# Five buffers for the exponentials of an attention block, with two small tiles moved into a shared region

## The chip, the cores and the metric

The kernel runs on one core of one Trainium2 chip. The metric is the device time of one execution in microseconds; three executions of the kernel before took 1975.81, 1975.38 and 1973.5, median 1975.38. A further execution was profiled: its time was 1972.27 and the span of its trace 1970.2.

## The reference, cut to what matters

The kernel computes one transformer block in which attention and the feed-forward part both read the normalized input. The input is 2048 tokens of 512 values; there are 16 heads of width 32; the feed-forward part has 4096 hidden units with weights packed in 4 bits.

```python
xn = _layernorm(x, axis=-1)
# attention
q, k, v = split(einsum('bsh,oh->bso', xn, w_qkv))      # 16 heads of 32
scores  = einsum('bhqd,bhkd->bhqk', q, k) / sqrt(32)
scores  = where(causal, scores, finfo.min)
probs   = softmax(scores, axis=-1)
attn    = einsum('bhqk,bhkd->bhqd', probs, v)
# feed-forward
inter   = gelu(xn @ Wg.T) * (xn @ Wu.T)
x = x + attn @ w_o.T + inter @ Wd.T
```

## The kernel before, in words

The kernel has an order of instructions written out by hand: each engine executes its instructions in the order in which the Python code issues them, and buffers are handed on by semaphore waits. Three stages follow each other.

**Projection and first maxima (0 to about 187 us).** The 16 token tiles of x are loaded, normalized (`normalize`, L489, into the tiles xn), turned with the identity matrix (`flip`, L505) and projected to q, k and v. Row maxima of the scores of the first two head pairs are taken.

**Attention, a pair of heads at a time (about 188 to 718 us).** Heads go in pairs, pair 0 to pair 7. For pairs 0 to 5 a loop runs over 40 steps a pair. A query block has 512 columns; the order of blocks is 1, 2, 3, 0, and block b has 4b + 4 key tiles of 128 rows. So steps 0 to 7 of a pair are block 1, steps 8 to 19 block 2, steps 20 to 35 block 3 and steps 36 to 39 block 0. Within a block the last four key tiles are diagonal: 4 to 7, 16 to 19, 32 to 35 and 36 to 39. Key tile 4 of block 2 is step 12, key tiles 4 and 8 of block 3 are steps 24 and 28. In each step, in this order:

- `score_cols` (L281) starts the scores of two heads in two PSUM banks of the pool ps_t (three banks) with the negated row maxima; `score_rows` (L210) computes scores of a later pair in two banks of ps_s (three banks); `add_scores` (L296) adds the products of keys and queries.
- `run_due` issues the values matmuls that earlier steps have put off (`add_values` L344, `add_rows` L355). `later_on` says by how many steps: for four full-width key tiles 0 to 3 in a row, the values of tile 0 are last read four steps after it was made.
- `exponentials` takes exp on ScalarE (ACT) from ps_t into a prob tile: two instructions of L310 in a full-width step. In a diagonal step the diagonal 128 columns are first clipped into the tile clip (L316), the rest goes to prob directly (L318), the clipped part is exponentiated into prob (L320) and `omit_later_keys` (L325) zeroes what lies above the diagonal on GpSimd (POOL).
- `maxima` (L234, L229) takes row maxima of the ps_s scores on VectorE (DVE), which frees these banks.
- `add_up` (L396, POOL) sums two prob tiles, so that row sums need half the matmuls. `keep_attention` (L430, L434 on ACT) copies a finished block out; `normalize_attention` issues one reciprocal (L445, DVE) and one product (L447, POOL) a step, up to four steps long, after a finished pair of pairs.

Some steps also hold a projection for a later group of heads (`project`, L166): eight matmul instructions of 3.7 us together, in steps 26, 28 and 30 of pairs 1 and 3 and in steps 5, 6, 14, 16 and 26 of pairs 2 and 4.

Pairs 6 and 7 run together (718 to 834 us, `exponentials_together`, L647), two prob tiles a step.

**Output projection and feed-forward (from about 834 us).** Pools of this part take the place of the attention's pools in SBUF, so some of its first loads wait for the last readers there. The SyncE queue issues all loads in order.

**Buffers.** prob comes from the pool probs with four buffers of 4 KB a partition, taken in turn; clip from a pool of its own with two buffers; the identity matrix ident from the pool of constants. A separate region, `turns`, holds 16 slots of 2 KB a partition with one buffer each, named by number: the tiles of x are in slots 0 to 7, the value weights in 8 to 11, the normalized tiles xn of the layer norm in 12 and 13; later the pair sums (`added`) are in 0 to 7, `both` in 8 and 9, and in the run of pairs 6 and 7 the low parts of the tokens in 0 to 15.

```python
tc.tile_pool(name="probs", bufs=4) as probs,
tc.tile_pool(name="clip", bufs=2) as clipp,
...
def turn_tile(i, name, dtype=F32, shape=(P, TB)):
    return turns.tile(list(shape), dtype, tag=f"turn{i}", name=name)
```

Of the kernel before, what the change touches and what calls it, by code (L numbers as in the profile page):

```python
# [38 lines left out]
F32 = mybir.dt.float32  # L39
# [7 lines left out]
P = 128  # L47
# [31 lines left out]
def block_kernel(  # L79
# [15 lines left out]
    def turn_tile(i, name, dtype=F32, shape=(P, TB)):  # L95
        return turns.tile(list(shape), dtype, tag=f"turn{i}", name=name)
# [17 lines left out]
    with (  # L114
# [3 lines left out]
        tc.tile_pool(name="vals", bufs=1) as vals,  # L118
        tc.tile_pool(name="tops", bufs=6) as topsp,
        tc.tile_pool(name="neg", bufs=8) as negp,  # L120
        tc.tile_pool(name="probs", bufs=4) as probs,
        tc.tile_pool(name="sums", bufs=5) as sump,
        tc.tile_pool(name="clip", bufs=2) as clipp,
        tc.tile_pool(name="qk", bufs=10) as qkp,
        tc.tile_pool(name="ps_s", bufs=3, space=PSUM) as ps_s,
        tc.tile_pool(name="ps_t", bufs=3, space=PSUM) as ps_t,
        tc.tile_pool(name="ps_m", bufs=1, space=PSUM) as ps_m,
    ):
        ident = const.tile([P, P], F32, tag="ident", name="ident")
        make_identity(nc, ident)  # L130

        mask_qk = const.tile([P, TB], F32, tag="mask_qk", name="mask_qk")
# [171 lines left out]
        def exponentials(p, n, tiles):  # L304
            qb, kt = steps[n]
            c0 = max(0, kt - 4 * qb) * P
            prob = probs.tile([P, 2, TB], F32, tag="prob", name=f"prob{p}_{n}")
            if kt < 4 * qb:
                for h, ps in enumerate(tiles):
                    nc.scalar.activation(prob[:, h, :], ps, AF.Exp)  # L310
                return prob


            clip = clipp.tile([P, 2, P], F32, tag="clip", name=f"clip{p}_{n}")
            for h, ps in enumerate(tiles):
                nc.scalar.activation(clip[:, h], ps[:, c0 : c0 + P], AF.Relu, scale=-1.0)  # L316
                if c0 + P < TB:
                    nc.scalar.activation(prob[:, h, c0 + P :], ps[:, c0 + P :], AF.Exp)  # L318
            diag = prob[:, :, c0 : c0 + P]
            nc.scalar.activation(diag, clip, AF.Exp, scale=-1.0)  # L320
            omit_later_keys(diag)
            return prob

        def omit_later_keys(diag):
            nc.gpsimd.affine_select(  # L325
                out=diag,
                in_=diag,
                compare_op=ALU.is_ge,
                fill=0.0,
                base=0,  # L330
                pattern=[[0, 2], [1, P]],
                channel_multiplier=-1,
            )
# [201 lines left out]
        for b in range(NTB):  # L535
            n = first[b]
# [34 lines left out]
        for m in range((NP - 2) * STEPS):  # L571
            p, n = divmod(m, STEPS)
# [7 lines left out]
            add_scores(p, n, ps)  # L580
            run_due(m)
            prob = exponentials(p, n, ps)
            maxima(ahead, n, ps_max)
            while full:
# [51 lines left out]
        def exponentials_together(p, n, tiles):  # L636
            if not diagonal(n):
                return exponentials(p, n, tiles)
            qb, kt = steps[n]
            c0 = (kt - 4 * qb) * P  # L640
            prob = probs.tile([P, 2, TB], F32, tag="prob", name=f"prob{p}_{n}")
            for h, ps in enumerate(tiles):

                nc.vector.tensor_scalar(
                    ps[:, c0 : c0 + P], ps[:, c0 : c0 + P], 0.0, None, ALU.min
                )
                nc.scalar.activation(prob[:, h, c0:], ps[:, c0:], AF.Exp)  # L647
            omit_later_keys(prob[:, :, c0 : c0 + P])
            return prob
# [433 lines left out]
```

## Time and profile before

| | us |
|---|---|
| median of three runs | 1975.38 |
| time of the profiled execution | 1972.27 |
| span of its trace | 1970.2 |
| TensorE busy / weight loads busy | 1934.5 / 1182.9 |
| VectorE / ScalarE / GpSimd busy | 1326.7 / 1104.2 / 927.6 |
| attention of pairs 0 to 5 | 188 to 718 |
| attention of pairs 6 and 7 | 718 to 834 |

A profile page gives the busy time of each engine, shares in slices, a chain of waits that ended last, and groups of instructions by line. Besides the page the trace answers questions: a table of waits (who waited for whom, in total, how often, the longest), and a timeline in order of time with start, length, engine, line, tile and form. In a timeline line, "x2" marks two like instructions drawn as one, and the square bracket tells how long the engine was idle before and what ended that. PE is TensorE, PEld its weight loads, DVE VectorE, ACT ScalarE, POOL GpSimd. The start of a matmul is recorded; its end is modelled.

### The profile page before, as it was taken

Reading aid. Unit: us, or ns where it says so; the run is one execution under the profiler, and the core shown is the slowest. Engines: PE = TensorE matmul, PEld = TensorE weight load, DVE = VectorE, ACT = ScalarE, POOL = GpSimd, SP = SyncE. Lnnn points to the kernel's source line nnn. Section 1 sums busy time; section 2 is a strip of 40 time slices with the busy share of each in tenths; the row PEclk is TensorE's granted clock in tenths of the full one; section 3 lists DMA queues with packets and bytes.
Section 4 is the critical chain, followed back from the end, with each engine's and each line's share of the span. In section 5 each row is a group of like instructions: output and inputs, shape, how many; then the busy total and the mean of one; then the engine's idle time right before and its main releaser. Section 6 shows DMA issues by size and latency. Waiting matters only on the chain.

```text
span 1970.2 us, 32411 instructions
## 1 busy us (share of the span) xinstructions
PE 1934.5 (98%) x11648; PEld 1182.9 (60%) x11648; DVE 1326.7 (67%) x2706; ACT 1104.2 (56%) x2299; POOL 927.6 (47%) x1055
## 2 busy tenths in 40 slices
PE   7999999999999999999999999999999999999998
PEld 3433333333333332247888888888888888888886
DVE  5657665656555764187777676777777777777774
ACT  2112665656556666625666666666666666666664
POOL 1001555545445653155655454555555555555451
PEclk9999999999999999999999999999999999999999
DMA  3000000000000000020000000000000000000002
GB/s 128 0 11 11 2 2 1 1 12 2 1 1 12 2 1 21 18 79 22 22 18 23 19 22 20 21 20 20 19 22 20 21 21 21 21 19 24 18 5 86
DMA packets 55392, 39.86 MB, mean 20 GB/s; under 512 B 14784, under 2 KB 47552, under 8 KB 55232
## 3 DMA queue, kind: packets, MB, share of 16 engines
q1 hardware_dynamic: 55232, 37.81, 6.5%
q8 instruction: 91, 1.49, 0.3%
q14 instruction: 69, 0.57, 0.1%
HBM read 33.55 MB, written 4.19 MB: 19 GB/s over the span
## 4 chain that ended last, share of the span: by engine, by line
PE 94%; ACT 3%; POOL 1%; issue 1%; DVE 1%; DMA 0%; DVEq 0%; ACTq 0%; POOLq 0%
PE gu L935 24%; PE gu L948 12%; PE pd L998 12%; PE av L344 10%; PE ps_s L210 8%; PE pd L1010 6%; PE ps_qk L166 6%; PE ps_t L281 4%; PE ps_t L296 3%; PE ps_v L516 3%; PE po L890 3%; ACT prob L310 2%; POOL added L396 1%; PE ptx L505 0%; PE pm L262 0%
## 5 line engine op out<-in xcount | busy, mean ns | idle before, releaser
L935 PE MATMUL gu<-xh,gu 128*128 128x512 f32 x1024 | 403.9, 394 | 0.0
L935 PE MATMUL gu<-lm,gu 128*128 128x512 f32 x1024 | 403.7, 394 | 0.0
L234 DVE TENSOR_REDUCE tops<-ps_s 128x1 f32<-128x512 f32 x384 | 243.7, 682 | 160.4 <-PE ps_s L210 122.3
L1019 DVE SCALAR_TENSOR_TENSOR acc<-pd,acc 128x512 f32<-128x512 f32 x512 | 317.1, 682 | 2.4 <-PE pd L1010 2.4
L980 POOL TENSOR_TENSOR parts<-inter,hi 128x512 fp32r<-128x512 f32 x128 | 171.1, 1336 | 278.2 <-DVE hi L976 271.9
L310 ACT ACTIVATE prob<-ps_t 128x512 f32<-128x512 f32 x384 | 205.7, 596 | 145.6 <-PE ps_t L296 102.1
L210 PE MATMUL ps_s<-qk,qk 32*128 32x512 f32 (+3 forms) x1280 | 286.4, 576 | 0.0
L948 PE MATMUL gu<-lm,gu 128*128 128x512 f32 x1024 | 279.7, 395 | 0.0
L972 DVE SCALAR_TENSOR_TENSOR inter<-gu,gate 128x512 f32<-128x512 f32 x128 | 88.5, 692 | 274.9 <-PE gu L948 274.9
L296 PE MATMUL ps_t<-qk,qk 32*128 32x512 f32 (+3 forms) x1280 | 271.2, 538 | 0.0
L1005 ACT ACTIVATE pd<-pd 128x512 f32<-128x512 f32 x512 | 263.4, 583 | 1.1 <-PE pd L998 1.1
L344 PE MATMUL av<-prob,v 128*32 128x128 f32 (+3 forms) x1856 | 257.6, 425 | 5.5 <-ACT both L430 4.2
L998 PE MATMUL pd<-wd,parts 128*128 128x512 f32 x1024 | 259.6, 396 | 0.0
L942 ACT ACTIVATE gu<-gu 128x512 f32<-128x512 f32 x256 | 148.7, 581 | 188.2 <-PE gu L935 188.1
L396 POOL TENSOR_TENSOR added<-prob,prob 128x512 f32<-128x512 f32 x144 | 179.6, 1268 | 115.9 <-ACT prob L310 115.4
L948 PEld LDWEIGHTS gu<-lm,gu 128*128 128x128 f32 x1024 | 192.0, 188 | 47.1 <-issue 0.2
L935 PEld LDWEIGHTS gu<-lm,gu 128*128 128x128 f32 x1024 | 191.9, 187 | 46.6 <-POOL wd L805 0.2
L998 PEld LDWEIGHTS pd<-wd,parts 128*128 128x128 f32 x1024 | 192.3, 188 | 45.8
L935 PEld LDWEIGHTS gu<-xh,gu 128*128 128x128 f32 x1024 | 192.0, 188 | 45.7 <-ACT wd L804 0.2
L344 PEld LDWEIGHTS av<-prob,v 128*32 128x32 f32 x1856 | 67.2, 108 | 206.2 <-issue 147.5
L229 DVE CUSTOM_DVE_ANT_0 ps_s<-ps_s,mask_qk 128x128 f32<-128x128 f32 (+3 forms) x256 | 120.8, 516 | 92.0 <-PE ps_t L296 52.3
L979 ACT CAST parts<-hi 128x512 fp32r<-128x512 f32 x128 | 79.7, 623 | 173.2 <-DVE hi L976 171.4
(106 smaller groups left out, 2942.8 us busy)
## 6 DMA issues: line engine op xcount, KB each, us to landing
pk<-packed SPq DMA_DIRECT2D x96, 128.0 KB, 2.2
sc<-scales SPq DMA_DIRECT2D x512, 8.0 KB, 1.6
x<-x SPq DMA_DIRECT2D x16, 256.0 KB, 3.5
acc<-x SPq DMA_DIRECT2D x16, 256.0 KB, 3.3
sc<-scales SPq DMA_DIRECT2D x256, 16.0 KB, 1.7
out<-acc SPq DMA_DIRECT2D x16, 256.0 KB, 2.2
wqk<-w_qk SPq DMA_DIRECT2D x4, 512.0 KB, 3.7
wv<-w_v SPq DMA_DIRECT2D x4, 256.0 KB, 5.4
```

The costliest lines, as they stand in the source:

```text
L210: nc.tensor.matmul(ps[:, :w], lhsT=qT[p // 2, qb][rows, i * P : (i + 1) * P], rhs=kT[p // 2, c][rows, :w], start=True, stop=True,)
L234: nc.vector.tensor_reduce(top, ps[:, :w], AX.X, ALU.max)
L296: nc.tensor.matmul(ps[:, c0:], lhsT=kT[p // 2, kt // 4][rows, (kt % 4) * P : (kt % 4 + 1) * P], rhs=qT[p // 2, qb][rows, c0:], start=False ...
L310: nc.scalar.activation(prob[:, h, :], ps, AF.Exp)
L344: nc.tensor.matmul(avs[p, qb][D * j : D * (j + 1), c0:c1], lhsT=v[kt // 4][:, kt % 4, D * head : D * (head + 1)], rhs=prob[:, h, c0:c1], s ...
L396: nc.gpsimd.tensor_tensor(t, prob_a[:, h], prob_b[:, h], ALU.add)
L935: nc.tensor.matmul(ps, lhsT=parts[:, i, k], rhs=mov, start=(k == 0 and i == 0), stop=(k == NK - 1 and i == 1),)
L948: nc.tensor.matmul(ps, lhsT=gu[g, m, j][:, 2, k], rhs=lm[b, k][1], start=False, stop=(k == NK - 1), skip_group_check=True,)
L980: nc.gpsimd.tensor_tensor(parts[:, 1], inter, high, ALU.subtract)
L998: nc.tensor.matmul(po, lhsT=parts[:, part, i * P : (i + 1) * P], rhs=w[:, part], start=(part == 0), stop=(part == 1),)
L1005: nc.scalar.activation(po, po, AF.Copy, scale=HIGH_SCALE)
L1019: nc.vector.scalar_tensor_tensor(acc[t], po, SUM_SCALE, acc[t], ALU.mult, ALU.add)
```

## The change

The pool of the exponentials gets a fifth buffer, and two small tiles leave their pools. The clipped scores use turn slots 12 and 13 by the parity of the step, where the normalized tiles xn of the layer norm were; the pool clip is gone. The identity matrix uses turn slot 14. The rest of the program, and the order of instructions on each engine, is the same.

```diff
-        tc.tile_pool(name="probs", bufs=4) as probs,
+        tc.tile_pool(name="probs", bufs=5) as probs,
         tc.tile_pool(name="sums", bufs=5) as sump,
-        tc.tile_pool(name="clip", bufs=2) as clipp,
...
-        ident = const.tile([P, P], F32, tag="ident", name="ident")
+        ident = turn_tile(14, "ident", shape=(P, P))
...
-            clip = clipp.tile([P, 2, P], F32, tag="clip", name=f"clip{p}_{n}")
+            clip = turn_tile(12 + n % 2, f"clip{p}_{n}", shape=(P, 2, P))
```

## The prediction

> **What bounds the kernel now.** I read the page first, then the table of waits for the stretch 186 to 720 us (pairs 0 to 5), then the timeline of single steps, because the first two turned out not to show the stall that matters.
>
> ```profile
> PE 1934.5 (98%) x11648; PEld 1182.9 (60%) x11648; DVE 1326.7 (67%) x2706; ACT 1104.2 (56%) x2299; POOL 927.6 (47%) x1055
> ```
>
> TensorE is busy 98% of the span at a granted clock of 0.999, so whatever the change brings must come out of TensorE's time. The two tiles that the change touches, prob and clip, live between 190 and 834 us; after that TensorE is busy without a gap (24.00 of 24.00 us from 836 to 860, 100.00 of 100.00 from 900 to 1000), so later stages only move along.
>
> ```profile
> ACT prob L310 <- PE av L344: 23.3, 18, 1.4
> ACT prob L310 <- POOL added L396: 16.5, 19, 0.9
> PE ps_t L281 <- ACT prob L310: 2.3, 3, 1.2
> ```
>
> These are idle us, times, and the longest. The first row is the wait that a fifth buffer can end: the exponentials of a step wait for the last values matmuls that read the buffer of four steps before. 18 times is 6 pairs by 3: key tile 4 of block 2, and key tiles 4 and 8 of block 3 (a quad's first tile is read until four steps later). The third row suggests that TensorE hardly cares. It is misleading, as the timeline of steps 28 and 29 of pair 0 shows (start, length, engine, line):
>
> ```profile
> 244.41 0.39 PE L281 MATMUL ps_t<-neg,ones_h 3*128 3x512 bf16 x2
> 245.07 0.59 PE L296 MATMUL ps_t<-qk,qk 32*128 32x512 f32 x2
> 246.05 0.39 PE L344 MATMUL av<-prob,v 128*32 128x256 f32 x2
> 246.11 1.09 ACT L310 ACTIVATE prob<-ps_t 128x512 f32<-128x512 f32 x2 [1.24 <-PE av L344]
> 246.38 0.75 PE L281 MATMUL ps_t<-neg,ones_h 3*128 3x512 bf16 x2
> 246.76 0.70 PE L210 MATMUL ps_s<-qk,qk 32*128 32x512 f32 x2
> 248.71 0.39 PE L281 MATMUL ps_t<-neg,ones_h 3*128 3x512 bf16 x2
> ```
>
> A step runs from one L281 pair to the next: 1.97 us for step 28, 2.33 for step 29. In step 28 the exponentials start 1.70 us after L281; in a step without the wait it is 1.34 (below: 332.10 to 333.44), so they are 0.36 late. The second L281 of step 29 takes the score bank that the first of these exponentials frees: ps_t has three banks, a step uses two. It starts 0.38 late, seen as a length of 0.75 instead of 0.39 and an L210 0.38 behind. Matmul ends are modelled, so this stall stands as busy time and is in no wait row. Now pair 1, where a projection of 3.7 us covers the same late exponentials:
>
> ```profile
> 328.46 3.70 PE L166 MATMUL ps_qk<-xnT,wqk 128*128 128x512 f32 x8
> 332.10 0.39 PE L281 MATMUL ps_t<-neg,ones_h 3*128 3x512 bf16 x2
> 333.44 1.08 ACT L310 ACTIVATE prob<-ps_t 128x512 f32<-128x512 f32 x2 [0.65 <-PE ps_t L296]
> 334.06 0.39 PE L281 MATMUL ps_t<-neg,ones_h 3*128 3x512 bf16 x2
> ```
>
> Step 29 is 1.96 us here: the trace of before contains the step without the stall. The first diagonal step of a block has it in a smaller form, since only the second instruction, L318, writes the prob tile:
>
> ```profile
> 300.34 0.28 ACT L316 ACTIVATE clip<-ps_t 128x128 f32<-128x128 f32 x1 [0.83 <-PE ps_t L296]
> 300.76 0.49 ACT L318 ACTIVATE prob<-ps_t 128x384 f32<-128x384 f32 x1
> 301.03 0.59 PE L281 MATMUL ps_t<-neg,ones_h 3*128 3x384 bf16 x2
> 302.98 0.28 PE L281 MATMUL ps_t<-neg,ones_h 3*128 3x256 bf16 x2
> ...
> 404.91 0.34 PE L281 MATMUL ps_t<-neg,ones_h 3*128 3x384 bf16 x2
> 406.62 0.28 PE L281 MATMUL ps_t<-neg,ones_h 3*128 3x256 bf16 x2
> ```
>
> Step 17 takes 1.95 us in pair 1 and 1.71 in pair 2, where a projection again covers the wait.
>
> [...]
>
> **The change part by part.** The sum is made against the profiled execution: span 1970.2, time 1972.27. The median of the runs is 1975.38, 3.1 above it; I carry the difference over.
>
> *Five prob buffers.* The order of instructions on every engine stays; only waits move: a tile waits for the readers of the tile five steps before instead of four. That work ends a whole step earlier at every place above, so ACT starts as soon as its scores are there (L296 plus 0.08). Then the second L281 is free within 0.02 to 0.03, as in steps without the wait. What is late next is VectorE: the second L210 takes the ps_s bank that the maxima of the step before free.
> - Full-width steps, VectorE early: step 13 of pair 0, step 25 of pairs 0, 2, 4, step 29 of pairs 0, 2, 4, 5: 8 x 0.36 = 2.9 us. (Step 29 of pairs 1 and 3 is covered already: 0.)
> - Step 13 of pairs 2 and 4: a reciprocal delays the maxima, so that L210's bank comes 0.15 after the step's start: 2 x 0.23 = 0.46.
> - Steps 13 and 25 of pairs 1, 3, 5: the same, with further reciprocals behind:
>
> ```profile
> 315.20 0.94 DVE L445 RECIPROCAL sums<-sums 128x128 f32<-128x128 f32 x1
> 316.06 1.22 DVE L234 TENSOR_REDUCE tops<-ps_s 128x1 f32<-128x512 f32 x2
> ```
>
>   Step 25 begins at 316.60 and the first maximum ends at 316.74 (0.68 each), so 0.23 is the upper end. VectorE is then a chain of maxima and reciprocals that does not get earlier, and the next two steps give back up to 0.2: lower end 0.03. I take 0.1, nearer to the chain: 6 x 0.1 = 0.6.
> - First diagonal steps: step 17 of pairs 0, 1, 3, 5 and step 33 of all six, 10 x 0.25 less 0.08 where VectorE is close = 2.4; step 5 of pairs 0, 1, 3, 5, 4 x 0.25 = 1.0; of pairs 2 and 4, VectorE bound, 2 x 0.07 = 0.14.
>
> Sum 2.9 + 0.46 + 0.6 + 2.4 + 1.0 + 0.14 = 7.5 us. Its lower end is 4.1 (the VectorE places at nothing, and 0.1 us lost again at each of the other 22, as L281's spread of 0.03 and VectorE's 0.06 together allow); its upper end is every stall whole: 16 x 0.38 + 16 x 0.27 = 10.4.
>
> *Pairs 6 and 7* (718 to 834 us) use two buffers a step and read them in the next step, before the exponentials that reuse them; no row there shows ACT waiting for L344. 0, and at most the 4.5 us in which L281 waits for exponentials there (3.1 and 1.4).
>
> *Clip in turn 12 and 13, ident in turn 14.* Same instructions. The clip tile's first wait is for the layer norm's last reader of these slots, over at 121.5 us, against 198.1 for the first clip; ident is written at 0.8 us into a fresh slot; low token parts enter these slots after 720 us, after the last clip at 716. Cover is over 4 us everywhere. Other tiles move in SBUF: L310 has 576 to 619 ns over four addresses now, so an address is worth less than 0.02 us an instruction either way, off the path: 0.
>
> *Waits elsewhere.* ACT loses 9 separate wait instructions and POOL 20, of 17 ns, beside other work: 0 to 0.5 us of gain, I take 0. Of the SyncE queue's transfers, one scale load before the feed-forward part waits for a prob buffer one step earlier (832.68 now); behind it queue accumulator loads, first needed over 10 us later. TensorE has no gap there: 0 either way. 18 weight loads of L281 get a wait for TensorE's own count; see the second rival.
>
> Result: 1972.27 - 7.5 = 1964.8 for a profiled execution, 1975.38 - 7.5 = **1967.9** for the median.
>
> **The rivals.** A difference below 0.2% (3.95 us) can't be told from none here.
>
> 1. *The score banks are the limit, not the prob buffers.* If exponentials were late for another reason (three ps_t banks, ACT's own queue), nothing changes: 1975.4. For it: what TensorE waits for is a PSUM bank. Against: in step 28 ACT is idle from 244.87, its scores end at 245.66 (245.07 + 0.59), and yet it starts only at 246.11, behind the L344 group that reads the old buffer. Half true would be where VectorE takes the stall over in most places: gain 2 to 4, 1972. [...]
>
> 2. *Slower: the new waits in TensorE's queue.* Each of 18 L281 weight loads waits for a score matmul of the step before. If such a wait emptied TensorE's pipeline, it would cost the score group in flight, 1.25 us from L281 to L296's end: 18 x 1.25 = 22.5, less 7.5: 1990. It decides from 0.64 us each, (7.5 + 3.95) / 18. Against: L210's weight loads wait for VectorE in every step and where that is over (244.43) they start without a gap; the matmul waited for ends about 0.7 us before the load is due (1.25 into a step of 1.97).
>
> 3. *Much faster: the second wait row too.* If ACT's waits for POOL were buffer waits, another 16.5 us would go: 1951. Against, the timeline of step 22 of pair 1:
>
> ```profile
> 310.35 0.68 PE L296 MATMUL ps_t<-qk,qk 32*128 32x512 f32 x2
> 311.11 1.09 ACT L310 ACTIVATE prob<-ps_t 128x512 f32<-128x512 f32 x2 [0.87 <-POOL added L396]
> ```
>
>   ACT starts 0.08 after its scores end at 311.03: the POOL end at 311.09 is a coincidence.
>
> **How the numbers follow.** Forecast (gain 4 to 10): 0.75. Rival 1: 0.16, of which 0.04 lies just over the 0.2% bound. Rival 2: 0.05. Rival 3: 0.04. Faster 0.75 + 0.04 + 0.04 = 0.83, same 0.16 - 0.04 = 0.12, slower 0.05. Range: from 1965.0 (the upper end of the sum, 10.4) to 1972.2 (into rival 1's half-true case), which leaves out under 2 in 10.
>
> **What would show it.** Right: step 29 of pair 0 at 1.97 us instead of 2.33, step 17 of pair 1 at 1.71; the row of ACT waiting for L344 gone; VectorE waits of L210 a little longer; gain spread evenly over pairs 0 to 5, none after 720 us. Wrong: step 29 still at 2.33, a gap before L281's weight loads in steps 5, 17 and 33, or the time before 186 or after 720 us changed.

## The result and the profile after

Six executions of the changed kernel have a median of 1966.26 us (1963.04 to 1968.42), six of the kernel before 1975.73 us: a ratio of 0.9954, with a 95% interval of 0.9944 to 0.9963. The forecast was 1967.9 with a range of 1965.0 to 1972.2. The profiled execution took 1963.04 us with a span of 1961.3 (before: 1972.27 and 1970.2). In the trace the line numbers below line 123 are one less than before, so L280, L209, L295, L309, L343 are the old L281, L210, L296, L310, L344.

The page again shows TensorE busy for 98% of the span. Its busy time fell by 8.6 us, though the change removes no matmul: what went was waiting that had stood inside the busy row.

```profile
PE 1925.9 (98%) x11648; PEld 1181.8 (60%) x11648; DVE 1325.1 (68%) x2706; ACT 1102.9 (56%) x2299; POOL 928.0 (47%) x1055
```

From the table of waits of the changed kernel for 185 to 715 us (idle us, times, longest):

```profile
ACT prob L309 <- PE ps_t L295: 97.7, 112, 1.2
...
ACT prob L309 <- POOL added L395: 14.7, 17, 0.9
...
PEld ps_s L209 <- DVE tops L233: 11.1, 35, 1.2
```

The row in which the exponentials waited for the values matmuls is gone. They now wait for their scores (L295), which is what should end last. The row with POOL is still there at 14.7 us: it was a coincidence, as the third rival's counter-argument said. The wait of L209's weight loads for VectorE, which was expected to grow a little, did not: 11.1 us in 35 waits, before 11.9 in 33.

For step 28 of pair 0 one line of the kernel before has to be added to those of the prediction: the group of L344 that reads the buffer of step 24 has 128 columns, and its last record ends, by the model, at 246.02, 0.09 ahead of the exponentials of 246.11.

```profile
245.59 0.63 PE L344 MATMUL av<-prob,v 128*32 128x128 f32 x10
```

The timeline of steps 28 and 29 of pair 0 in the changed kernel:

```profile
243.12 0.40 PE L280 MATMUL ps_t<-neg,ones_h 3*128 3x512 bf16 x2
...
243.78 0.60 PE L295 MATMUL ps_t<-qk,qk 32*128 32x512 f32 x2
...
244.31 0.63 PE L343 MATMUL av<-prob,v 128*32 128x128 f32 x10
...
244.46 1.08 ACT L309 ACTIVATE prob<-ps_t 128x512 f32<-128x512 f32 x2 [0.88 <-PE ps_t L295]
...
245.10 0.39 PE L280 MATMUL ps_t<-neg,ones_h 3*128 3x512 bf16 x2
...
247.06 0.39 PE L280 MATMUL ps_t<-neg,ones_h 3*128 3x512 bf16 x2
```

In step 28 the exponentials start at 244.46, 0.08 after their scores end (243.78 + 0.60) and 1.34 after the step began; before, it was 1.70. They no longer wait for L343: the group that reads the buffer of step 24 starts at 244.31 and its last record ends at 244.73, behind the start of the exponentials. The L280 of step 29 has its plain length of 0.39 again, and step 29 takes 1.96 to 1.97 us instead of 2.33. Step 17 of pair 1, a diagonal step, in the same view:

```profile
298.48 0.28 ACT L315 ACTIVATE clip<-ps_t 128x128 f32<-128x128 f32 x1
...
298.64 0.51 ACT L317 ACTIVATE prob<-ps_t 128x384 f32<-128x384 f32 x1
298.64 0.33 PE L280 MATMUL ps_t<-neg,ones_h 3*128 3x384 bf16 x2
...
300.34 0.28 PE L280 MATMUL ps_t<-neg,ones_h 3*128 3x256 bf16 x2
```

L317 follows L315 by 0.16 instead of 0.42, and the step takes 1.70 instead of 1.95. Before, only pairs 2 and 4 had that, under the cover of a projection.

The step lengths of the whole stage, from one L280 pair to the next, give the account. "Given back" is what the following steps became longer. No step outside this table changed by more than 0.05 us.

| place | instances | before, us | after, us | net gain, us |
|---|---|---|---|---|
| step 13 of pair 0; 25 of 0, 2, 4; 29 of 0, 2, 4, 5 | 8 | 2.33 | 1.97 | 2.9 |
| step 13 of pairs 2, 4 | 2 | 2.33 | 2.01 | 0.6 (0.03 each given back) |
| steps 13 and 25 of pairs 1, 3, 5 | 6 | 2.33 | 2.01 | 1.5 (0.03 to 0.09 each given back) |
| step 17 of pairs 0, 1, 3, 5; step 33 of all | 10 | 1.96 | 1.70 to 1.76 | 2.4 |
| step 5 of pairs 0, 1, 3, 5 | 4 | 1.96 (pair 0: 2.18) | 1.70 (1.91) | 1.0 |
| step 5 of pairs 2, 4 | 2 | 5.59 | 5.53 | 0.1 |
| step 9 of pair 3, a lone wait | 1 | 2.04 | 1.75 | 0.3 |
| all 240 steps | | 528.44 | 519.62 | 8.8 |

By pairs the gain is 1.83, 1.24, 1.32, 1.51, 1.32 and 1.59. Pairs 6 and 7 changed by 0.01 and the time after them by 0.02. Outside the span lie 1.74 us instead of 2.07: 8.9 of the span and 0.3 from there make the 9.2 between the two profiled executions; the medians are 9.5 apart.

### The profile page after: what moved, and what is told of

Read it like the earlier page. It is cut to its first block, busy times and chain, and to the rows that moved or that the text cites. A ratio compares the mean times of both kernels' runs of the same rounds, so it can differ in the third digit from the quotient of the medians.

```text
span 1961.3 us, 32383 instructions
## 1 busy us (share of the span) xinstructions
PE 1925.9 (98%) x11648; PEld 1181.8 (60%) x11648; DVE 1325.1 (68%) x2706; ACT 1102.9 (56%) x2299; POOL 928.0 (47%) x1055
## 4 chain that ended last, share of the span: by engine, by line
PE 94%; ACT 3%; POOL 1%; issue 1%; DVE 1%; DMA 0%; DVEq 0%; ACTq 0%; POOLq 0%
PE gu L934 24%; PE gu L947 12%; PE pd L997 12%; PE av L343 10%; PE ps_s L209 9%; PE pd L1009 6%; PE ps_qk L165 6%; PE ps_t L280 4%; PE ps_t L295 3%; PE ps_v L515 3%; PE po L889 3%; ACT prob L309 2%; POOL added L395 1%; PE ptx L504 0%; PE pm L261 0%
## 5 line engine op out<-in xcount | busy, mean ns | idle before, releaser
L209 PE MATMUL ps_s<-qk,qk 32*128 32x512 f32 (+3 forms) x1280 | 288.6, 576 | 0.0
L309 ACT ACTIVATE prob<-ps_t 128x512 f32<-128x512 f32 x384 | 205.9, 596 | 138.4 <-PE ps_t L295 121.5
L295 PE MATMUL ps_t<-qk,qk 32*128 32x512 f32 (+3 forms) x1280 | 266.9, 537 | 0.0
L343 PE MATMUL av<-prob,v 128*32 128x128 f32 (+3 forms) x1856 | 257.6, 425 | 5.5 <-ACT both L429 4.2
L343 PEld LDWEIGHTS av<-prob,v 128*32 128x32 f32 x1856 | 67.2, 108 | 206.2 <-issue 148.3
```

Source lines behind the costliest of these rows:

```text
L209: nc.tensor.matmul(ps[:, :w], lhsT=qT[p // 2, qb][rows, i * P : (i + 1) * P], rhs=kT[p // 2, c][rows, :w], start=True, stop=True,)
L295: nc.tensor.matmul(ps[:, c0:], lhsT=kT[p // 2, kt // 4][rows, (kt % 4) * P : (kt % 4 + 1) * P], rhs=qT[p // 2, qb][rows, c0:], start=False ...
L343: nc.tensor.matmul(avs[p, qb][D * j : D * (j + 1), c0:c1], lhsT=v[kt // 4][:, kt % 4, D * head : D * (head + 1)], rhs=prob[:, h, c0:c1], s ...
```

## The experiments

### The moves without the fifth buffer

```diff
-        tc.tile_pool(name="probs", bufs=5) as probs,
+        tc.tile_pool(name="probs", bufs=4) as probs,
```

> Four prob buffers, with clip and ident in the turn slots as in the change. Theory (the fifth buffer alone brings the gain): time as before, 1975.7 within 1.5 us; step 29 of pair 0 at 2.33 us, step 17 of pair 1 at 1.96, and ACT's wait for L344 back at 18 times and 23 us. Rival (the gain comes from where the tiles lie in SBUF or from the fewer wait instructions): 1966, step 29 at 1.97.

Measured: 1975.26 us (1972.41 to 1976.42), against 1974.99 for the kernel before in the same series; ratio 1.0 [0.999, 1.0009]. The step lengths that had fallen are back at their old values; only step 9 of pair 3 stays at 1.76. The wait row is back (18 waits and 23 us were expected), and so is the late start in step 28 of pair 0 (wait table, then timeline, of this kernel):

```profile
ACT prob L309 <- PE av L343: 21.9, 17, 1.4
```

```profile
247.36 0.39 PE L280 MATMUL ps_t<-neg,ones_h 3*128 3x512 bf16 x2
...
249.06 1.08 ACT L309 ACTIVATE prob<-ps_t 128x512 f32<-128x512 f32 x2 [1.24 <-PE av L343]
...
249.33 0.75 PE L280 MATMUL ps_t<-neg,ones_h 3*128 3x512 bf16 x2
...
251.66 0.39 PE L280 MATMUL ps_t<-neg,ones_h 3*128 3x512 bf16 x2
```

1.70 us into the step, an L280 of 0.75, a step of 2.33: the numbers of before. The new places of clip and ident and the shifted addresses cost and bring nothing; the gain comes with the fifth buffer. One part of the rival is not tested here: the smaller number of wait instructions also comes with the fifth buffer. ACT and POOL have 684 and 786 of them in this trace, 682 and 786 before, and 673 and 766 in the changed kernel. Against it speaks the table above, in which the steps that became shorter are, but for one, the stalled ones.

### The last reader a step earlier, with four buffers

The same wait can be ended from the other side: the old buffer's last read comes one step sooner, in the kernel before.

```diff
-                    later_on(3, attend_pair, p, n - 1, even, prob, 3 * P, TB)
+                    later_on(2, attend_pair, p, n - 1, even, prob, 3 * P, TB)
```

> The kernel before with four prob buffers; only the last values matmuls that read the first tile of a quad are issued one step earlier (three steps after the tile was made instead of four), so that the old buffer is free when its successor comes. Theory (it is this one reader that holds the buffer): steps 13, 25 and 29 of pair 0 fall from 2.33 to about 1.97, steps 5, 17 and 33 by about 0.25; with 0.3 us of matmuls moved from one step to the one before, the time comes to 1964 to 1969. Rival (a fifth buffer also ends other waits, those for POOL among them, or the score banks are the limit): 1973 to 1976.

Measured: 1969.86 us (1966.73 to 1972.04), ratio 0.9978 [0.9967, 0.9988]; 1964 to 1969 was expected. The wait for L344 is gone, so this reader did hold the buffer, yet less came than with the fifth buffer. The timeline of steps 28 and 29 of pair 0 shows where the rest stayed:

```profile
246.87 0.39 PE L281 MATMUL ps_t<-neg,ones_h 3*128 3x512 bf16 x2
...
248.21 1.09 ACT L310 ACTIVATE prob<-ps_t 128x512 f32<-128x512 f32 x2 [1.11 <-PE ps_t L296]
...
248.62 0.61 PE L281 MATMUL ps_t<-neg,ones_h 3*128 3x512 bf16 x2
...
250.81 0.39 PE L281 MATMUL ps_t<-neg,ones_h 3*128 3x512 bf16 x2
```

ACT is on time (1.34 into the step). But the moved matmuls took 0.22 us of TensorE's work out of step 28, which is now 1.75 long, and put it into step 27. ACT's pace has not changed: the first exponential frees its score bank some 1.95 us after the step's start. So the next L281 finds its second bank 0.22 late (a length of 0.61 instead of 0.39), and step 29 takes 2.19. A step with less work than that loop only waits in the next one. This is the score-bank limit of the first rival: real, but at about 1.97 us a step, just where the changed kernel's steps already are.

The small stalls show the same: steps 5, 17 and 33 fell from 1.96 to 1.93 only, where 0.25 less was expected. By the step lengths (without the first five steps of pair 0, where TensorE had about half its clock for a while, 0.66 on average from 190 to 200 us, see the last section) the stage is 5.6 us shorter than before. Only 2.0 of that is in steps 13, 25 and 29; 3.5 is in the fourth and fifth steps of the blocks, where the moved matmuls fill a wait of another kind. So the experiment shows what the exponentials waited for, but not what the wait was worth.

### The last reader a step later, with five buffers

```diff
-                    later_on(3, attend_pair, p, n - 1, even, prob, 3 * P, TB)
+                    later_on(4, attend_pair, p, n - 1, even, prob, 3 * P, TB)
```

> The changed kernel with five prob buffers; the last values matmuls that read the first tile of a quad are issued one step later (five steps after), which puts the same wait back, one step further on. Theory: ACT waits for L344 again; the stall of 0.36 to 0.38 us moves to steps 14, 26 and 30 (step 30 of pair 0 from 1.97 to about 2.33), the small one to steps 6, 18 and 34; time 1971 to 1976. Rival (five buffers help whoever reads last): 1966, no step longer than in the changed kernel.

Measured: 1975.23 us (1972.13 to 1976.06), ratio to before 1.0001 [0.9992, 1.0011]. The fifth buffer is cancelled, as expected. From the wait table of this kernel:

```profile
ACT prob L309 <- PE av L343: 22.2, 18, 1.5
```

The total came out, the division by steps only in part: steps 13, 25 and 29 without a projection take 2.39 to 2.44, since the moved 0.22 and the late bank meet there, and the steps behind them 2.10 to 2.11 and not 2.33: the long step has taken up most of the delay of its exponentials. The small stall did not move to steps 6, 18 and 34, which stayed at 1.43; steps 5, 17 and 33 take 2.13 where nothing else holds them, instead of 1.70. And as the moved matmuls leave the fifth steps of the blocks, those are shorter, so the near agreement of the total with the kernel before is in part chance. What these three experiments show is the wait itself: it goes and returns with the number of steps between a buffer's last read and its next use, from either side.

### VectorE's reciprocals apart from the late maxima

The prediction gave the odd pairs little since reciprocals stand among the maxima. Here the reciprocals of a finished block start no earlier than its sixth step:

```diff
-            if invert and kt < 4 * qb:
+            if invert and 5 <= kt < 4 * qb:
```

> The changed kernel; the reciprocals and products of finished blocks are issued only from key tile 5 of a block on, not at key tiles 0 to 4. Theory (where a reciprocal stands between two maxima, VectorE hands on the ps_s bank late and holds TensorE): step 24 of pairs 1, 3, 5 falls from 2.56 to about 2.26, step 12 of pairs 2 and 4 from 2.47 to 2.26, step 4 of pairs 2 and 4 from 2.58 to 2.12, and steps 13 and 25 of the odd pairs from 2.01 to 1.97; the steps that get the reciprocals grow by up to 0.04 each; sum -2.5 to -4 us, time 1962 to 1964. Rival (ScalarE's late exponentials set these steps anyway): 1966, step 24 of pair 1 still at 2.56.

Measured: 1962.04 us (1961.23 to 1962.9), ratio to before 0.9936 [0.9922, 0.9951], inside the expectation, and so is the stage by its step lengths, 3.3 us shorter than in the changed kernel. Step 13 and 25 of the odd pairs went from 2.01 to 1.97, so VectorE had only 0.04 left there. The larger part came in the step ahead: step 4 of pairs 2 and 4 from 2.58 to 2.12, step 12 of these pairs from 2.47 to 2.26. In the odd pairs, steps 12 and 24 went from 2.56 to 2.40 only, where 2.26 was expected: something else holds them too.

### The second copy of a finished block two steps later

In the fourth step of a block ACT has two copies (L429, L433) between the exponentials of two steps. The second copy and POOL's addition behind it are deferred, in the changed kernel:

```diff
-                    nc.scalar.copy(aT[og][qb][half], both[other])
-                    nc.gpsimd.tensor_tensor(
-                        aT[og][qb][half], aT[og][qb][half], both[half], ALU.add
-                    )
+                    later_on(2, join_halves, p, qb, both)
+                    return
...
+        def join_halves(p, qb, both):
+            nc.scalar.copy(aT[og][qb][half], both[other])
+            nc.gpsimd.tensor_tensor(
+                aT[og][qb][half], aT[og][qb][half], both[half], ALU.add
+            )
+            if p % 2 == 1:
+                invert.extend((og, qb, i) for i in range(4))
```

> Changed kernel, but ScalarE's second copy of a finished block (L434) and GpSimd's addition behind it come two steps later, so that in the fourth step of a block only one copy stands between the exponentials of two steps. Theory (ScalarE hands the score banks over late in that step, and VectorE's reciprocals are not what makes the fourth step of a block and the next one long): the 18 fourth steps (2.71 us now) become 0.2 to 0.4 us shorter and step 12 and 24 of pairs 0, 2, 4 (2.26) come near 1.97; 18 x 0.3 = 5.4 us, median 1959 to 1963. Rival (VectorE or the matmuls themselves set these steps): the copy is idle time on an engine that is not the bound, and the copy that comes two steps later delays exponentials there: 1966, or up to 2 us more.

Measured: 1959.73 us (three executions at 1959.71 to 1959.74, one at 1965.01), ratio to before 0.9932 [0.9915, 0.995]. Steps 23 and 24 of pair 1, first in the changed kernel:

```profile
308.68 0.81 PE L280 MATMUL ps_t<-neg,ones_h 3*128 3x512 bf16 x2
...
310.06 0.62 ACT L433 COPY aT<-both 64x512 f32<-64x512 f32 x1
...
310.70 1.08 ACT L309 ACTIVATE prob<-ps_t 128x512 f32<-128x512 f32 x2
...
311.39 0.82 PE L280 MATMUL ps_t<-neg,ones_h 3*128 3x512 bf16 x2
...
313.96 0.42 PE L280 MATMUL ps_t<-neg,ones_h 3*128 3x512 bf16 x2
```

and then with the copy deferred:

```profile
308.14 0.81 PE L280 MATMUL ps_t<-neg,ones_h 3*128 3x512 bf16 x2
...
309.88 1.08 ACT L309 ACTIVATE prob<-ps_t 128x512 f32<-128x512 f32 x2 [0.39 <-PE ps_t L295]
...
310.85 0.54 PE L280 MATMUL ps_t<-neg,ones_h 3*128 3x512 bf16 x2
...
312.96 0.39 PE L280 MATMUL ps_t<-neg,ones_h 3*128 3x512 bf16 x2
```

The exponentials of step 23 start 1.74 after the step's start instead of 2.02, the L280 of step 24 is 0.54 instead of 0.82 long, and step 24 takes 2.11 instead of 2.57. The median is as expected, but the place is not: the fourth steps (308.14 to 310.85) stayed as they were in all 18 instances (2.71, and 3.19 in step 3 of pair 0), so ACT's copies don't set them. One part of their length shows in both traces: the second L280 of this step starts 0.43 behind the first (0.91 in step 3 of pair 0), before either copy begins. In the second trace that is at 308.57, 0.05 behind the first exponential of step 22, whose single record ends at 308.52. Steps 21 and 22 take 1.75 and 1.76, less than the 1.97 of the loop of exponential and score bank, and the lag ends up here. What sets the rest of the step was not tried.

The size came in part by luck. By the step lengths the stage is 3.5 us shorter than in the changed kernel, where 5.4 was expected. The medians differ by 6.5, since three of these four executions have a mean clock of 1.0 and only two of the six of the changed kernel have; between executions at 1.0 (1959.71 and 1963.05) it is 3.3.

The edit also holds back the reciprocals of these blocks, which wait behind the deferred addition. The share of the copy alone is the difference between the version with late reciprocals and the version with both (below): 0.14 us in steps 12 and 24 of even pairs, 0.28 in odd ones, 2.6 in all.

### The table of the exponential loaded early

Executions of one kernel come in groups some 2 to 3 us apart (the six of the changed kernel at 1963.04 and 1963.06, 1966.24 to 1966.31, and 1968.42), which a gain of 9 us has to be told from. The last section deals with the cause; this edit tests it. A tiny exponential is put ahead, so that its function table isn't loaded at 188.7 us, where the load takes 1.28 us and TensorE sits idle for 1.19. First it was put among the projections (behind the layer norm's last statistics), in the changed kernel and in the kernel before:

```diff
+            if b + 2 == NTB:
+                warm_exp = small.tile([P, 1], F32, tag="warm_exp", name="warm_exp")
+                nc.scalar.activation(warm_exp, ones[:, :1], AF.Exp)
```

> Changed kernel plus one tiny exponential (128x1) on ScalarE right after the layer norm's last statistics, so that the table of the exponential is loaded there, under the projections, and not at 188.8 us, where its 1.28 us stand on the path while TensorE has nothing to do. Theory A (the gap at the load is what halves TensorE's clock for 6.827 us in some executions, at about 2.7 us each time): the load leaves 188.8 us, the stage starts 1.2 to 1.3 us earlier, and no execution has the stretch, so that the runs lie together near 1962 instead of in clusters at 1963.0, 1966.3 and 1968.4; median 1961 to 1963. Rival B (the stretch comes whatever stands there): the load's 1.3 us go and the clusters stay, median near 1965. Rival C (the load is hidden by other waits): 1966.3, no difference.

> The kernel before, with the early load of the exponential's table alone. Theory A (gap at the load triggers the half clock): 1971 to 1972 without clusters, and the ratio to the changed kernel with the same edit gives the gain of the fifth buffer without that noise: 8.8 us by the step lengths. Rival B: 1974 with clusters. Rival C: 1975.5, no difference.

Measured: 1964.93 us (1964.17 to 1965.23) for the changed kernel with it, 1973.89 (1972.74 to 1975.6) for the kernel before with it; ratios to before 0.9949 [0.9934, 0.9964] and 0.9995 [0.9985, 1.0004]. Both medians missed theory A (1961 to 1963, and 1971 to 1972) and came out at rival B's numbers; the clocks, in the last section, are what speaks for A. The two differ by 8.96 us, which is the gain of the change once more. Step 1 of pair 0 fell from 2.54 to 1.82, but the load is on the path at its new place as well. Timeline of the changed kernel with the load among the projections:

```profile
83.72 1.28 ACT L541 ACT_TABLE_LOAD   x1
...
85.12 0.58 ACT L177 ACTIVATE qk<-ps_qk 128x512 f32<-128x512 f32 x1
...
85.75 0.70 PE L165 MATMUL ps_qk<-xnT,wqk 128*128 128x512 f32 x1 [1.96 <-ACT qk L177]
```

So the load was then put where ACT is idle for 4.3 us, just ahead of the last copy of a projection:

```diff
                     n += 1
+                    if b == NTB - 1 and i == 3 and j == b:
+                        warm_exp = small.tile([P, 1], F32, tag="warm_exp", name="warm_exp")
+                        nc.scalar.activation(warm_exp, ones[:, :1], AF.Exp)
```

> Changed kernel with the tiny exponential in a place where ScalarE is idle for 4.3 us (between the last copy of value products, 183.2 us, and the last copy of a projection, 188.1 us), so that the table load costs nothing there, as it did cost 1.1 to 1.25 us among the projections at 83.7 us. Theory A (the table load makes the gap in TensorE's work near 189 us, and without the gap the half clock does not come): stage starts as in the changed kernel, step 1 of pair 0 is 1.82 instead of 2.54 and the step before it about 0.7 shorter, so 1961.6 where the changed kernel had 1963.05; mean clock 0.999 or 1.0 in every run, none of the levels at 1966.3 and 1968.4. Theory B (the early load of the last batch shifted the stage or changed something else, and the half clock went away for that reason): clocks of 0.998 and 0.997 in about half of the runs again, median 1964 to 1966.

Measured: 1963.2 us (1962.72 to 1965.66), ratio to before 0.9946 [0.9933, 0.9958]; 1961.6 was expected of an execution like the profiled one, and that one took 1963.2. Its step 1 is 0.72 shorter and nothing is lost at the new place, but the first L280 came 0.6 later than in the profiled execution of the changed kernel, and lone waits of 0.28 and 0.26 stand at step 3 of pair 4 and step 29 of pair 5 (the first is given back in the next step). All four traces of the changed kernel with an early load have them at these two steps; what they are is open. In four traces whose code is the same up to there, that of the changed kernel among them, the stage starts between 187.99 and 189.46 us, so 0.6 is within that scatter.

### All three together

> The changed kernel with three edits together: reciprocals not before the sixth step of a block, the table of the exponential loaded early, and the second copy of a finished block two steps later. If the three gains stand in different steps they add: 4.2 (measured alone) + 1.3 to 4 + 0 to 5.4 from 1966.3, so 1954 to 1960. If the later copy and the later reciprocals free the same wait in step 12 and 24, some 1 to 2 us of it is lost: 1958 to 1962.

> The three edits together (reciprocals from the sixth step, second copy two steps later, table load), with the table load in that gap of ScalarE instead of among the projections. By the step lengths: 1959.5 of the version with the load among the projections less 1.1 to 1.25 for the load's cost there: 1958.3, runs between 1956 and 1959.5. Theory B of the other kernel: half of the runs 2.7 us later, median 1959 to 1961.

Measured: 1959.49 us (1958.47 to 1960.42) with the load among the projections, ratio to before 0.9922 [0.9907, 0.9937]; 1958.01 us (1957.44 to 1958.55) with the load in ACT's idle time, 0.9918 [0.9904, 0.9931], the best of all kernels here. Both are inside the expectations. Against the changed kernel the stage is 6.0 us shorter by the step lengths: 4.0 in steps 12 and 24, 1.3 in steps 4 and 5 of pairs 2 and 4, 0.7 in step 1 of pair 0, and the rest small amounts of both signs. Steps 12 and 24 take 2.12 in all pairs. Alone the edits gave 3.3, 3.5 and 0.7 by the step lengths, 7.5 in sum. The two lone waits, which these traces have too, take 0.5 of that; some 1 us is freed by the later copy and by the later reciprocals alike, as the first expectation had it in its second half.

## Why the prediction was right, and where it was off

- **What bounds the kernel.** Right: the stall was in TensorE's busy row (down by 8.6 us), not in the 2.3 us of the wait row. By that row the time would have been 1973.1 (1975.38 less 2.3). It doesn't stand in the length of a single record: the two L281 of step 29 last 0.38 and 0.37, the second starts 0.38 behind the first, and the modelled end of the first covers the wait.
- **Full-width steps with VectorE early, 8 x 0.36.** Measured 8 x 0.36.
- **First diagonal steps, 2.4 + 1.0 + 0.14.** Measured 2.4, 1.0 and 0.12.
- **Steps 13 and 25 of the odd pairs, 6 x 0.1.** This is the term that was mis-sized: it measured 6 x 0.25, 1.5 instead of 0.6; step 13 of pairs 2 and 4 was 0.29 instead of 0.23. The prediction took the step as held by the ps_s bank that the first maximum frees about 0.15 after its start, and as the upper end let that delay through in full. Step 25 of pair 1 in the changed kernel shows what happens:

```profile
313.42 1.22 DVE L233 TENSOR_REDUCE tops<-ps_s 128x1 f32<-128x512 f32 x2
...
313.96 0.42 PE L280 MATMUL ps_t<-neg,ones_h 3*128 3x512 bf16 x2
...
314.01 0.79 PE L209 MATMUL ps_s<-qk,qk 32*128 32x512 f32 x2
...
314.56 0.94 DVE L444 RECIPROCAL sums<-sums 128x128 f32<-128x128 f32 x1
```

  The maxima are as late as before against the step: they start 0.54 ahead of it. But the first instruction of the L209 pair starts at once, at 314.01: there are three ps_s banks, and one is free. Only the second waits for the first maximum, whose single record ends at 314.05; it starts at 314.11. The pair is 0.79 long instead of 0.70, and the step loses 0.04 in all (2.01 instead of 1.97). Nor did the "chain of maxima and reciprocals" give the gain back: 0.03 to 0.09 in the steps behind, not up to 0.2. That 0.04 is what the experiment with late reciprocals took away.
- **The lone wait in step 9 of pair 3 (0.28)** was not in the sum. Such a wait of 0.26 to 0.28 stands at other steps in other kernels' traces, with the moves alone at step 25 of pair 5, and at none in that of the changed kernel. Why it is gone there is not shown.
- **Clip, ident, other addresses: 0.** Confirmed together by the kernel with the moves alone, 1.0 [0.999, 1.0009]. **Waits elsewhere: 0.** These come with the fifth buffer, so that kernel says nothing of them; that no step outside the table changed by more than 0.05, and the time after pair 7 by only 0.02, agrees with 0.
- **Rival 1, score banks.** False at the stalled steps, where ACT's late start was the cause. The experiment with the earlier read shows the limit that it spoke of, at 1.97 us a step.
- **Rival 2, slower by the new waits of L281's weight loads.** Steps 5, 17 and 33 are the ones with such waits, and where nothing else holds them they take 1.70 us, as long as the covered steps of before. The waits cost nothing that can be seen.
- **Rival 3, much faster.** The POOL row is still there with 14.7 us, at steps of full speed.
- **Two slips of the working.** The line of L344 that it shows for step 28, at 246.05 with 256 columns, reads the buffer of step 26; the group that reads the old one is that of 245.59 above, and the argument holds with it. And what the range leaves out is 0.12 + 0.05 + 0.04 = 0.21, a little over 2 in 10.
- **The 3.1 us carried over to the median.** The same distance came out after the change, 1966.26 less 1963.04. That is in part luck, since it depends on how many of six executions had the lower clock (four, 0.997 to 0.999).

Sum: 8.5 of the 8.8 us are the predicted places; 7.5 was forecast, and 0.9 of the difference is the odd pairs' term. Another 0.3 of the 9.2 between the profiled executions lies outside the span, for which the sum had no term.

## What to carry to other kernels

A matmul row that is busy 98% of the time can hold stalls (8.6 us of them here): compare the lengths of steps that should be alike, and look for a neighbour in which the same work is shorter. When an engine waits for a PSUM bank, follow the chain to the engine that should free it, and ask what that engine waits for; here it was a buffer in SBUF, and its worth was the number of steps in which the wait ended last, times the delay against an unstalled step. With three ps_s banks for two users, the late bank delayed only the second (314.11, the first at 314.01) and cost the step 0.04 us, so bound such a term by the user that really waits.

## What the runs showed of the hardware

**A half-clock stretch in the middle of some executions.** In the profiled execution of the kernel with the moves alone, TensorE's granted clock is low for one stretch early in the attention. Windows of the changed kernel first, then of that one (us, then the busy time and instructions of PE, PEld, DVE, ACT and POOL, then the granted clock, the DMA share and GB/s):

```profile
190.00:200.00 10.00, 8.28 (x81) 3.48 (x80) 5.71 (x11) 6.83 (x15) 5.34 (x5) 1.00 0.10 37
```

```profile
190.00:200.00 10.00, 8.08 (x45) 2.95 (x48) 4.72 (x8) 4.83 (x10) 3.98 (x5) 0.66 0.11 42
```

The clock of the second is 0.66 here and 1.00 in the ten us before and behind. In the slow stretch the second pair of L209 of step 2 starts 1.02 us behind the first (193.97 and 192.95), 0.53 in the changed kernel (193.07 and 192.54): about half the rate. At half, a mean of 0.66 over ten us is a stretch of some 6.8 us, an estimate from that mean. Steps 2 and 3 of pair 0 take 2.80 and 4.97 us there instead of 1.90 and 3.19: 2.7 us, which is about what separates the executions of this kernel with a mean clock of 1.0 (1972.41 to 1972.73) from those with 0.998 (1975.21 to 1976.42). In the changed kernel the match is less clear: of three executions near 1966.3 two have a mean clock of 0.999. Ahead of the first slow matmuls, at 192.95 us, TensorE has two gaps in the kernel with the moves alone: 1.19 us up to 191.05, and 0.54 up to 192.95. The larger one comes behind the table load (189.11 us, 1.28 long). Timeline of the changed kernel, and below it the one with the table load in ACT's idle time:

```profile
188.70 1.28 ACT L309 ACT_TABLE_LOAD   x1
...
189.99 1.09 ACT L309 ACTIVATE prob<-ps_t 128x512 f32<-128x512 f32 x2
...
190.64 0.37 PE L280 MATMUL ps_t<-neg,ones_h 3*128 3x512 bf16 x1 [1.19 <-ACT prob L309]
```

```profile
184.39 1.28 ACT L557 ACT_TABLE_LOAD   x1
...
189.88 1.09 ACT L309 ACTIVATE prob<-ps_t 128x512 f32<-128x512 f32 x2 [0.59 <-PE ps_t L295]
...
190.53 0.37 PE L280 MATMUL ps_t<-neg,ones_h 3*128 3x512 bf16 x1 [0.47 <-ACT prob L309]
```

Where the load stood at 188.7 us, 49 of 85 executions had a mean clock of 0.998 or less (6.8 us at half is 0.0017 of the span); with the load moved away, in five kernels and to two places, none of 28 did. So the low mean clocks come with the load at 188.7 us. That they come by its gap of 1.19 us, in place of 0.47, is the author's estimate from these counts: the gap was not tried apart from the load, and the changed kernel's own trace has the gap and no stretch. That the stretch is behind each of these mean clocks is not shown either: it was seen in two traces, those of the moves alone and of the earlier read. Not all of the spread is explained by it: the kernel before with the early load still lies between 1972.74 and 1975.6 at clocks of 0.999 and more.

**Time outside the span.** The time of the profiled execution exceeds its span by 2.04 to 2.09 us in the four kernels with four prob buffers and by 1.67 to 1.74 us in the eight with five. This 0.35 us is part of the gain; where it comes from was not tried.
